# Attention's shift as a 33rd row of the score products, in a one-core four-layer hybrid kernel

## The chip, the cores and the metric

The kernel runs on one core of a Trainium2 chip. The core's engines each execute their own list of instructions in order: TensorE (PE, with its weight loads shown as PEld), VectorE (DVE), ScalarE (ACT), GpSimd (POOL) and SyncE (SP), which here only issues DMAs. They meet at semaphores. The metric is the device time of one execution in microseconds; less is better. The kernel before takes 6303.35 us, the median of three runs (6299.39, 6303.35 and 6311.23). A single-core kernel has no other cores to wait for.

## What is computed

An image batch (4, 32, 32, 256) passes through four layers; each batch element is a sequence of 1024 tokens of 256 channels.

- Layer 0: layer norm, projection to 512 channels, 3x3 depthwise convolution, a selective scan with 64 states per channel, projection back, plus the residual.
- Layer 1: a bottleneck block: 1x1, grouped 3x3 and 1x1 convolution.
- Layer 2: attention over a graph (8 heads of 32 channels, 1024 queries, 1024 keys, a mask made of the edges), then a mixture of 8 experts.
- Layer 3: a selective scan with 16 states per channel, then a second mixture of experts.

What matters here is the attention's core. For every head, query n and key k:

```
s[n, k] = q[n] . k[k] / sqrt(32)          # 32 channels
p[n, k] = exp(s[n, k] + mask[n, k] - m[n])   # m: a shift per query and head
out[n]  = sum_k p[n, k] v[k] / sum_k p[n, k]
```

The result doesn't depend on m. It only has to keep the exponential in range. The kernel bounds all scores by the norms of q and k; when the bound is under 40 it leaves m at zero, and only otherwise enters a branch that takes the true row maxima. With the inputs of this case no row maxima (`ps_sn` products) appear in the trace: the branch is skipped.

## The kernel before

**The scans.** The backbone is `scans` (line 384): 8 scans (4 batch elements in layer 0 and 4 in layer 3) in the order of `SCANS` (line 32), in all 1280 *units* of 128 rows by 1024 steps. A unit is: SP loads `dA` (512 KB, line 497), ACT takes its exponential, PE spreads the input over the states (`ps_rep`, 2 products), DVE multiplies by B and scans (`h`), POOL multiplies by C, and PE sums over the states (`ps_y`, 8 records for every 2 units). There are 5 `dA` buffers, so that SP issues the load of unit k+4 when the scan of unit k-1 has ended; `ps_rep` has 2 PSUM buffers.

**The side stages.** Everything else is a list of stages (`STAGES`, line 34): four `front`, four `middle` (end of layer 0, layer 1, attention, first experts, start of layer 3) and four `last` (end of layer 3 and second experts). Each is a Python generator that yields after a small piece of work. `run` (line 620) writes the program: between the halves of every unit it advances the current stage by pieces; `advance` (line 598) takes one stage at a time, and a stage starts when the one before it has been written out and the scan that it needs is done. What a stage hasn't finished when a scan needs its results is written out with no scan beside it (`need`, line 583, which sets `self.alone`).

**The pacing.** How many pieces go into a unit is decided by a clock per engine, `Metered` (line 99), which adds an estimate for every instruction as it is written. Pieces are added while no engine's clock is ahead of VectorE's:

```
if max(clock.values()) > clock["vector"] + LEAD or self.advance() is None:
    break
```

The estimate of a product is `matmul_us` (line 78): 0.46 ns per column, four times that for float32, a quarter for outputs of at most 32 rows, and half where the contraction has at most 32 rows:

```
if out.shape[0] <= 32:
    return us / 4
return us / 2 if lhsT.shape[0] <= 32 else us
```

**Attention's core.** `attention` (line 1264) normalizes and turns the tokens, projects them to `qT` and `kT` (channels on the 128 partitions, two chunks of 4 heads), bounds the scores (`large_scores`), loads the mask, makes `v`, and enters `shift`, the skipped branch. `mT` is the negated shift, zeros here: in bfloat16, where rows 0 to 2 of each head's 32 hold three parts of the float32 number. `all_heads` (line 1328) then walks 64 *steps* per batch element: 2 halves of the queries, 4 pairs of heads, 8 blocks of 128 keys. `scores` of step n is written after `values` of step n-2. A step's `scores` makes, for the two heads of the pair, one float32 product of 32 rows each (`ps_sc<-qT,kT`), adds the shift with one bfloat16 product of 32 rows each (`ps_sc<-mT,onesb`: ones times `mT`), adds the mask with one bfloat16 product of 128 rows each, and ACT exponentiates. `values` makes 4 float32 products with 32 output rows. A float32 product is two records in the trace. The two heads of a pair lie on neighbouring 32-row strips of the array. Where attention runs with no scan beside it, scores go to the scans' PSUM tile and are named `ps_sx`.

The order on each engine is the order in which the program was written; all SP transfers of scans and stages share one list.

Of the kernel before, what the change touches and what calls it, by code (L numbers as in the profile page):

```python
# [8 lines left out]
F32 = mybir.dt.float32  # L9
BF16 = mybir.dt.bfloat16  # L10
I32 = mybir.dt.int32
AF = mybir.ActivationFunctionType
ALU = mybir.AluOpType
# [4 lines left out]
P = 128  # L18
NB = 4
L = 1024  # L20
TB = L // P
C = 256
DI = 512
DC = DI // P
HEADS, HD = 8, 32
# [52 lines left out]
def matmul_us(out, lhsT=None, rhs=None, **_):  # L78
    if lhsT is None:
        lhsT = out  # L80
    us = 0.46e-3 * columns(out)
    if lhsT.dtype != BF16:
        us = max(4 * us, 0.3)
    if out.shape[0] <= 32:
        return us / 4
    return us / 2 if lhsT.shape[0] <= 32 else us


def by_columns(per, fixed, of=0):
# [53 lines left out]
class Hybrid:  # L143
# [1092 lines left out]
    def prepare2(self, st):  # L1236

        nc, vec = self.nc, self.vec
        self.gamma, self.beta, self.bo = (self.rows("L2_attn_" + n) for n in ("gamma", "beta", "bo"))
        wo = self.weight(st, "L2_attn_Wo", 2)  # L1240
        yield
        ps = self.ps("ps_bo", (P, C))
        for k in range(2):
            nc.tensor.matmul(
                ps, lhsT=vec["L2_attn_bv"][:, k : k + 1].to_broadcast([P, P]), rhs=wo[:, k, :],
                start=(k == 0), stop=(k == 1),
            )
        nc.vector.tensor_tensor(self.bo, self.bo, ps, ALU.add)
        self.isq = 1.0 / float(HD) ** 0.5
        self.bq = self.const.tile([P, 2], F32, name="bq_")  # L1250
        nc.vector.tensor_scalar(self.bq, vec["L2_attn_bq"], self.isq, None, ALU.mult)

        byhead = st.tile([P, 4], F32, name="byhead4")
        nc.vector.tensor_reduce(
            byhead, self.ident.rearrange("p (h d) -> p h d", d=HD), AX.X, ALU.add
        )
        self.byhead = self.const.tile([P, 4, 8], F32, name="byhead")
        nc.vector.tensor_copy(self.byhead, byhead.unsqueeze(2).to_broadcast([P, 4, 8]))
        self.onesb = self.const.tile([P, P], BF16, name="onesb")
        nc.vector.memset(self.onesb, 1.0)  # L1260
        self.ones = self.const.tile([P, 32], F32, name="ones32")
        nc.vector.memset(self.ones, 1.0)

    def attention(self, b, tb):
        nc, tc, vec = self.nc, self.tc, self.vec
        with tc.tile_pool(name=f"at{b}", bufs=1, side="right") as op:
            xa = op.tile([P, TB, C], F32, name="xa")
            qT = op.tile([P, 2, L], F32, name="qT")
            kT = op.tile([P, 2, L], F32, name="kT")
            v = op.tile([P, TB, C], F32, name="v")  # L1270
            mT = op.tile([P, 2, L], BF16, name="mT")
            maskT = op.tile([P, TB, L], BF16, name="maskT")
            wo = self.weight(op, "L2_attn_Wo", 2)
            large = op.tile([1, 1], I32, name="large")
            nc.vector.memset(mT, 0.0)
            with tc.tile_pool(name=f"aa{b}", bufs=1, side="right") as fp:
                wq, wk, wv = (self.weight(fp, "L2_attn_" + n, 2) for n in ("Wq", "Wk", "Wv"))
                xT = fp.tile([P, 2, L], F32, name="xTa")
                yield from self.norm(fp, tb, TB, xa, "lnt")
                yield from self.turned(xa, TB, xT)  # L1280

                def project(item):
                    w, dst, bias, sc, c, g = item
                    ps = self.ps("ps_qk")
                    cols = slice(g * 512, (g + 1) * 512)
                    self.mm(ps, lambda k: w[:, k, c * P : (c + 1) * P], xT, 2, cols)
                    nc.scalar.activation(
                        dst[:, c, cols], ps, AF.Identity, bias=bias[:, c : c + 1], scale=sc
                    )

                yield from self.pipe(
                    [
                        (w, dst, bias, sc, c, g)
                        for w, dst, bias, sc in (
                            (wq, qT, self.bq, self.isq), (wk, kT, vec["L2_attn_bk"], 1.0)
                        )
                        for c in range(2) for g in range(2)
                    ],
                    project, cost=1.7,
                )  # L1300

                yield from self.large_scores(fp, qT, kT, large)
                for _ in self.mask_work:
                    pass
                nc.sync.dma_start(maskT, self.mem[("maskT",)].rearrange("j p f -> p j f"))

                def values(j):
                    ps = self.ps("ps_v", (P, 2, C))
                    for i in range(2):
                        m = 2 * j + i  # L1310
                        for k in range(2):
                            nc.tensor.matmul(
                                ps[:, i, :], lhsT=xT[:, k, m * P : (m + 1) * P], rhs=wv[:, k, :],
                                start=(k == 0), stop=(k == 1),
                            )
                    nc.scalar.copy(v[:, 2 * j : 2 * j + 2, :], ps)

                yield from self.pipe(range(TB // 2), values, cost=1.7)
            go = nc.values_load(large, engines=self.sides, min_val=0, max_val=1)
            tc.mark_branch_hint_location(f"large{b}", go, engines=self.sides)  # L1320
            yield from self.add_rows(xa, self.bo, TB)
            yield from self.add_rows(tb, self.beta, TB)
            with tc.tile_pool(name=f"ab{b}", bufs=1, side="right") as fp:
                yield from self.shift(fp, qT, kT, mT, maskT, go, f"large{b}")
            with tc.tile_pool(name=f"ac{b}", bufs=1, side="right") as fp:
                yield from self.all_heads(b, fp, tb, qT, kT, v, maskT, mT, xa, wo)

    def all_heads(self, b, fp, tb, qT, kT, v, maskT, mT, xa, wo):
        nc = self.nc

        def divided(raw, sums, c):
# [8 lines left out]
        halves = [  # L1340
            [fp.tile([P, 2, 512], F32, tag=t, name=t, bufs=2) for t in ("raw", "sums")]
            for _ in range(2)
        ]
        scores, values = self.heads(fp, halves, qT, kT, v, maskT, mT)
        for n in range(len(steps) + 2):
            if n >= 2:
                values(steps[n - 2])
# [69 lines left out]
    def row_max(self, fp, qT, kT, mT, mask):  # L1417
# [1 line left out]

        nc = self.nc  # L1420

        m3 = fp.tile([P, TB, HEADS, 32], BF16, name="m3")
        nc.vector.memset(m3, 0.0)
        mx = fp.tile([P, TB, HEADS, 2], F32, name="mx")
        got = {}
        yield 1.0
# [29 lines left out]
        )  # L1456
        m = fp.tile([P, TB, HEADS], F32, name="mneg")
        nc.vector.tensor_reduce(m, mx, AX.X, ALU.max, negate=True)
        for s in range(3):
            nc.vector.tensor_copy(m3[:, :, :, s], m)  # L1460
            if s < 2:
                nc.vector.tensor_tensor(m, m, m3[:, :, :, s], ALU.subtract)
        yield 1.0

        def turn(item):
            c, g = item
            ps = self.ps("ps_m3", dtype=BF16)
            for k in range(4):
                nc.tensor.transpose(
                    ps[:, k * P : (k + 1) * P],  # L1470
                    m3[:, 4 * g + k, 4 * c : 4 * c + 4, :].rearrange("p h s -> p (h s)"),
                    self.identb,
                )
            nc.scalar.copy(mT[:, c, g * 512 : (g + 1) * 512], ps)

        yield from self.pipe([(c, g) for c in range(2) for g in range(2)], turn, cost=0.8)

    def heads(self, fp, halves, qT, kT, v, maskT, mT):

        nc = self.nc
        got, acc = {}, {}

        def scores(step):
            nh, hp, kb = step
            qs = slice(nh * 512, (nh + 1) * 512)
            c, at = hp // 2, 64 * (hp % 2)
            alone = self.alone  # L1490
            if alone:
                both = self.scan_psum.tile([P, 2, 512], F32, tag="x", name="ps_sx", bufs=2)
                two = [both[:, i, :] for i in range(2)]
            else:
                two = [self.psum.tile([P, 512], F32, tag="s", name="ps_sc", bufs=2) for _ in range(2)]
            rows = [slice(at + 32 * i, at + 32 * i + 32) for i in range(2)]
            for i in range(2):
                nc.tensor.matmul(
                    two[i], lhsT=kT[rows[i], c, kb * P : (kb + 1) * P], rhs=qT[rows[i], c, qs],
                    start=True, stop=False,  # L1500
                )
            for i in range(2):
                nc.tensor.matmul(
                    two[i], lhsT=self.onesb[rows[i], :], rhs=mT[rows[i], c, qs],
                    start=False, stop=False,
                )
            got[step] = p = fp.tile([P, 2, 512], F32, tag="p", name="p", bufs=3)
            for i in range(2):
# [659 lines left out]
```

## Time and profile before

| what | value |
|---|---|
| median of three runs | 6303.35 us |
| profiled execution | 6294.21 us, its span 6292.5 us |
| mean granted TensorE clock | 0.842 |
| PE busy | 5142.7 us, 82% |
| DVE busy | 5032.7 us, 80% |
| POOL, ACT busy | 3825.9 us (61%), 3410.6 us (54%) |
| attention steps of elements 0, 1, 2 | 1400 to 1645, 2462 to 2704, 3826 to 4072 us |
| attention steps of element 3 | 5192 to 5234 us beside the last units of scan (3, 2), 5234 to 5388 us alone |
| stage `last 0` ends, `middle 2` begins | 3617.25 us, 3622.86 us |
| stage `last 1` ends, `middle 3` begins | 4985.39 us, 4990.77 us |

All times inside the execution are counted from the start of the span. All instructions that the pacing meters are recorded at line 131 of the helper, so they are told apart by their tiles: "ps_sc<-qT,kT" is what writes `ps_sc` from `qT` and `kT`, "32*128 32x512 f32 x4" is 4 records with 32 rows of weights, 128 columns, and a moving operand of 32 by 512. A view of stretches lists the busy time of each engine and its record count in each, then the granted clock, the DMA share and GB/s.

### The profile page before, as it was taken

Reading aid. Unit: us, or ns where it says so; the run is one execution under the profiler, and the core shown is the slowest. Engines: PE = TensorE matmul, PEld = TensorE weight load, DVE = VectorE, ACT = ScalarE, POOL = GpSimd, SP = SyncE. Lnnn points to the kernel's source line nnn. Section 1 sums busy time; section 2 is a strip of 40 time slices with the busy share of each in tenths; the row PEclk is TensorE's granted clock in tenths of the full one; section 3 lists DMA queues with packets and bytes.
Section 4 is the critical chain, followed back from the end, with each engine's and each line's share of the span. In section 5 each row is a group of like instructions: output and inputs, shape, how many; then the busy total and the mean of one; then the engine's idle time right before and its main releaser. Section 6 shows DMA issues by size and latency. Waiting matters only on the chain. (4 is left out here: it accounts for less than half of the span.)

```text
span 6292.5 us, 59823 instructions
## 1 busy us (share of the span) xinstructions
PE 5142.7 (82%) x20249; PEld 2117.1 (34%) x20249; DVE 5032.7 (80%) x4016; ACT 3410.6 (54%) x4299; POOL 3825.9 (61%) x1948
## 2 busy tenths in 40 slices
PE   5676785579798568979869969989689779997999
PEld 2122120132253122234225522244145332543566
DVE  5888898988898998889889988899889982317811
ACT  3565655345496435558638735567547544336621
POOL 2787768665586766568767756577867752006600
PEclk7687785589798668979969979979779889999989
DMA  3555555544355656445455576345545761027611
GB/s 109 160 158 167 165 175 185 159 150 136 113 173 177 194 165 170 132 128 191 159 178 174 182 179 165 119 150 195 174 156 179 208 161 48 19 73 184 166 34 34
DMA packets 347915, 934.97 MB, mean 149 GB/s; under 512 B 37748, under 2 KB 120256, under 8 KB 345984
## 3 DMA queue, kind: packets, MB, share of 16 engines
q1 hardware_dynamic: 344880, 928.38, 48.7%
q0 software_dynamic: 2128, 2.13, 0.2%
q8 instruction: 165, 2.70, 0.2%
q14 instruction: 166, 1.36, 0.1%
q10 hardware_dynamic: 576, 0.39, 0.0%
HBM read 841.02 MB, written 92.37 MB: 148 GB/s over the span
## 5 line engine op out<-in xcount | busy, mean ns | idle before, releaser
L131 POOL TENSOR_TENSOR h<-h,rows 128x1024 f32<-128x1024 f32 x1280 | 3024.2, 2366 | 1740.4 <-DVE h L131 1529.3
L131 DVE TENSOR_TENSOR_SCAN h<-dA,ps_rep 128x1024 f32<-128x1024 f32 x1280 | 2924.3, 2285 | 182.2 <-ACT dA L131 53.6
L131 DVE TENSOR_TENSOR ps_rep<-ps_rep,rows 128x1024 f32<-128x1024 f32 x1280 | 1549.4, 1210 | 142.6 <-PE ps_rep L131 141.7
L131 PE MATMUL ps_rep<-S,spread_L_conv_A_log 96*128 96x512 bf16 x2048 | 752.8, 456 | 770.3 <-DVE h L131 722.4
L131 ACT ACTIVATE dA<-dA,A_L_conv_A_log 128x1024 f32<-128x1024 f32 x1024 | 1125.4, 1142 | 440.0 <-DMA dA<-dt 405.7
L131 PE MATMUL ps_y<-h,collect_L_conv_A_log 128*32 128x512 f32 x4096 | 704.4, 741 | 15.3 <-POOL h L131 15.3
L131 PE MATMUL ps_e<-we,h_m 128*128 128x256 f32 x3072 | 709.4, 383 | 8.3 <-ACT h_m L131 8.3
L131 PEld LDWEIGHTS <-spread_L_conv_A_log 96*128 96x128 bf16 x2048 | 159.7, 102 | 1558.0 <-DVE h L131 1246.4
L131 PEld LDWEIGHTS ps_e<-we,h_m 128*128 128x128 f32 x3072 | 583.3, 191 | 159.2 <-ACT h_m L131 31.0
L131 PE MATMUL ps_h<-xTm,we 128*128 128x512 f32 x1280 | 603.3, 607 | 4.6 <-DMA we<-in_L_ffn_W_dram 4.5
L131 ACT ACT_TABLE_LOAD x402 | 515.8, 1283 | 37.0 <-PE ps_h L131 15.5
L131 ACT ACTIVATE h_m<-ps_h,cols 128x512 f32<-128x512 f32 x384 | 257.5, 686 | 423.0 <-PE ps_h L131 421.0
L131 ACT ACTIVATE p<-ps_sc 128x512 f32<-128x512 f32 x404 | 219.3, 594 | 316.7 <-PE ps_sc L131 306.1
L131 ACT ACTIVATE dA<-dA,A_L_attn_A_log 128x1024 f32<-128x1024 f32 x256 | 282.8, 1143 | 141.4 <-DMA dA<-dt 122.8
L131 PEld LDWEIGHTS ps_h<-xTm,we 128*128 128x128 f32 x1280 | 242.2, 193 | 281.0 <-issue 211.5
L131 PE MATMUL ps_rep<-S,spread_L_attn_A_log 96*128 96x512 bf16 x512 | 176.8, 433 | 160.2 <-DVE h L131 138.6
L131 PE MATMUL ps_at<-p,v 128*32 128x512 f32 x1024 | 270.7, 608 | 0.2 <-ACT p L131 0.2
L131 PE MATMUL ps_at<-p,ones 128*32 128x512 f32 x1024 | 270.7, 608 | 0.0
L131 DVE SCALAR_TENSOR_TENSOR tb_rows<-ps_e,cw,tb_rows 128x256 f32<-128x256 f32 x128 | 55.7, 477 | 242.8 <-PE ps_e L131 242.7
L131 PE MATMUL ps_sc<-qT,kT 32*128 32x512 f32 x808 | 244.0, 654 | 4.6 <-ACT p L131 2.0
L131 PE MATMUL ps_cv<-pad,diag 128*128 128x512 f32 x504 | 230.5, 597 | 0.0
L131 PEld LDWEIGHTS ps_y<-h,collect_L_conv_A_log 128*32 128x32 f32 x4096 | 93.2, 118 | 339.7 <-issue 216.6
(347 smaller groups left out, 5475.6 us busy)
## 6 DMA issues: line engine op xcount, KB each, us to landing
dA<-dt SPq DMA_DIRECT2D x1280, 512.0 KB
we<-in_L_ffn_W_dram SPq DMA_DIRECT2D x64, 512.0 KB
parts<-parts SPq DMA_DIRECT2D x60, 384.0 KB
S<-parts SPq DMA_DIRECT2D x90, 256.0 KB
dt<-sp_r SPq DMA_DIRECT2D x64, 256.0 KB
y<-yo SPq DMA_DIRECT2D x128, 128.0 KB
y_back<-y SPq DMA_DIRECT2D x64, 256.0 KB
we<-in_L_ffn_w_dram SPq DMA_DIRECT2D x64, 256.0 KB
```

The source lines that it names most:

```text
L131: return got(*args, **kw)
```

## The change

1. The shift becomes a 33rd row of the score product: k gets a row of ones, q a row that holds the negated shift in float32. The ones product, `onesb` and the three-part bfloat16 `mT` go. A step's `scores` is then two float32 products of 33 rows and the two mask products.
2. The heads' rows are laid out in DRAM: `k_rows` and `q_rows`, 33 rows of 1024 per head and batch element. In `prepare2` four transfers write the row of ones. In `attention` sixteen transfers of 32 rows by 1024 (128 KB) store q and k after the projections and before `large_scores`; one of 8 rows (32 KB) stores `mT` after the branch.
3. `heads` loads them back two heads at a time: `load` issues four transfers (two of 132 KB for k, two of 66 KB for q) into tiles where one head lies on partitions 0 to 32 and the other on 64 to 96, with two buffers. The first pair and the second are loaded in front of step 0, each later one a pair ahead.
4. `qT`, `kT` and `mT` live in an inner pool that is released before `all_heads`; the skipped branch makes 8-row transposes.
5. `matmul_us` halves the estimate for contractions of up to 64 rows, which the 33-row products alone meet besides those that had the half before.

```diff
-    return us / 2 if lhsT.shape[0] <= 32 else us
+    return us / 2 if lhsT.shape[0] <= 64 else us
...
-        self.onesb = self.const.tile([P, P], BF16, name="onesb")
-        nc.vector.memset(self.onesb, 1.0)
+        one = st.tile([HEADS, L], F32, name="one_row")
+        nc.vector.memset(one, 1.0)
+        self.k_rows = [self.keep(("k", b), [HEADS, HD + 1, L]) for b in range(NB)]
+        for to in self.k_rows:
+            nc.sync.dma_start(to[:, HD, :], one)
...
+                    for x, to in ((qT, self.q_rows(b)), (kT, self.k_rows[b])):
+                        for h in range(HEADS):
+                            at = HD * (h % 4)
+                            nc.sync.dma_start(to[h, :HD, :], x[at : at + HD, h // 4, :])
+                    yield from self.large_scores(fp, qT, kT, large)
...
                 with tc.tile_pool(name=f"ab{b}", bufs=1, side="right") as fp:
                     yield from self.shift(fp, qT, kT, mT, maskT, go, f"large{b}")
+                nc.sync.dma_start(self.q_rows(b)[:, HD, :], mT)
             with tc.tile_pool(name=f"ac{b}", bufs=1, side="right") as fp:
-                yield from self.all_heads(b, fp, tb, qT, kT, v, maskT, mT, xa, wo)
+                yield from self.all_heads(b, fp, tb, v, maskT, xa, wo)
...
+        def load(nh, hp):
+            k = fp.tile([P, L], F32, tag="k_rows", name="k_rows", bufs=2)
+            q = fp.tile([P, 512], F32, tag="q_rows", name="q_rows", bufs=2)
+            for i in range(2):
+                at = slice(64 * i, 64 * i + HD + 1)
+                nc.sync.dma_start(k[at, :], self.k_rows[b][2 * hp + i])
+                nc.sync.dma_start(q[at, :], self.q_rows(b)[2 * hp + i, :, nh * 512 : (nh + 1) * 512])
+            rows[nh, hp] = k, q
...
-            rows = [slice(at + 32 * i, at + 32 * i + 32) for i in range(2)]
+            if kb == 0:
+                at = 4 * nh + hp
+                for g in range(0 if at == 0 else at + 1, min(at + 2, 8)):
+                    load(g // 4, g % 4)
+            k, q = rows[nh, hp]
             for i in range(2):
+                of = slice(64 * i, 64 * i + HD + 1)
                 nc.tensor.matmul(
-                    two[i], lhsT=kT[rows[i], c, kb * P : (kb + 1) * P], rhs=qT[rows[i], c, qs],
-                    start=True, stop=False,
-                )
-            for i in range(2):
-                nc.tensor.matmul(
-                    two[i], lhsT=self.onesb[rows[i], :], rhs=mT[rows[i], c, qs],
-                    start=False, stop=False,
+                    two[i], lhsT=k[of, kb * P : (kb + 1) * P], rhs=q[of, :], start=True, stop=False
                 )
```

## The prediction

> **What bounds the kernel now.** I first read the page's slices.
>
> ```profile
> PE   5676785579798568979869969989689779997999
> ...
> DVE  5888898988898998889889988899889982317811
> ```
>
> VectorE is at 8 or 9 tenths, so the scans set the pace, except in the 34th to 36th slice and the last two: there it falls to 3 and less while PE stays at 9. The first of these gaps is the end of `middle 3`, which scan (3, 3) waits for; the second is the last experts. What shortens PE's work in the first is gained whole. Next the stretches (busy time of PE, PEld, DVE, ACT, POOL; then the clock, DMA share and GB/s).
>
> ```profile
> 1100.00:1220.00 120.00, 66.79 (x204) 7.79 (x204) 115.50 (x68) 39.31 (x35) 80.00 (x34) 0.50 0.53 166
> 1400.00:1645.00 245.00, 241.32 (x1376) 64.85 (x1380) 215.39 (x137) 140.04 (x207) 149.87 (x68) 0.99 0.41 130
> ...
> 5192.00:5234.00 42.00, 41.44 (x205) 10.96 (x204) 26.78 (x16) 17.96 (x29) 23.33 (x12) 0.81 0.24 58
> 5234.00:5388.00 154.00, 154.00 (x879) 38.90 (x871) 14.43 (x19) 64.92 (x73) 22.30 (x18) 1.00 0.14 33
> ```
>
> With no stage beside it a unit takes 120/34 = 3.53 us (34 scans lie in the first stretch), nearly all DVE. In attention PE is busy 241 of 245 us and DVE only 215: **in all four attentions PE is the bound**, beside the scans (second and third row) and alone (last). VectorE's groups in the second stretch give the pace:
>
> ```profile
> L131 DVE TENSOR_TENSOR_SCAN h<-dA,ps_rep 128x1024 f32<-128x1024 f32 x59 | 134.9, 2286 | 11.2 <-ACT dA L131 5.5 <-DVEq L1411 0.2
> ```
>
> 64 steps over 59 units: 1.085 steps a unit, 4.14 us a unit. Then PE in order of time, one step with no scan beside it:
>
> ```profile
> 5301.87 1.13 PE L131 MATMUL ps_sx<-qT,kT 32*128 32x512 f32 x4
> 5302.84 0.38 PE L131 MATMUL ps_sx<-mT,onesb 32*128 32x512 bf16 x2
> 5303.15 0.60 PE L131 MATMUL ps_sx<-maskT,identb 128*128 128x512 bf16 x2
> 5303.69 0.62 PE L131 MATMUL ps_at<-p,v 128*32 128x512 f32 x2
> ...
> 5304.68 0.70 PE L131 MATMUL ps_sx<-qT,kT 32*128 32x512 f32 x2
> ```
>
> From start to start: score pair 0.97 us, ones pair **0.31**, mask 0.54, values 0.99; a step is 2.81. And a unit's own share, beside a step:
>
> ```profile
> 1481.24 0.60 PE L131 MATMUL ps_rep<-S,spread_L_conv_A_log 96*128 96x512 bf16 x2
> 1481.77 1.13 PE L131 MATMUL ps_sc<-qT,kT 32*128 32x512 f32 x4
> ...
> 1483.58 1.06 PE L131 MATMUL ps_y<-h,collect_L_conv_A_log 128*32 128x512 f32 x8
> 1484.47 0.60 PE L131 MATMUL ps_at<-p,v 128*32 128x512 f32 x2
> ```
>
> 0.53 for `ps_rep` and 0.89 every second unit for `ps_y`: 0.97 a unit. Check: 64 x 2.81 + 59 x 0.97 = 237.0; the steps last 244.3 us (1400.6 to 1644.9), and the other 7.3 are the output projection and the cold start.
>
> **The ones product goes.** 0.31 us a step, 256 steps, all on PE where PE is the bound: 79 us at most.
>
> **The score pair gets 33 rows.** The trace has no product of 33 to 64 rows beside another. Its bounds: the 32-row pair, 0.97, where both heads run at once; and one after the other, 2 x 0.86 (a full float32 product: `ps_h` in the chain, 16 records in 6.87 us) + 0.12 = 1.84. No reading of the trace makes it cheaper than 0.97. The Trainium skill, TensorEngine Tiling (Array Packing), section Overview, gives contractions of up to 64 rows a factor of up to two, and its Tiling Modes list two tiles of 64 rows. Partitions 0 to 32 and 64 to 96 fall into different ones. By that rule the step becomes 2.50 us; without it 3.37. I take 0.97, the nearest row: it too has two heads on separate strips.
>
> **The pacing.** Its estimates by step were 0.94 (scores) + 0.24 (ones) + 0.47 (mask) + 0.94 (values) = 2.59; they become 2.35. With the new 64-row limit the pair keeps its half. So 1.085 x 2.59/2.35 = 1.19 steps go into a unit, and 64 steps take 54 units, five fewer. A unit's PE work is 0.97 + 1.19 x 2.50 = 3.95, still over 3.53: PE remains the bound.
>
> **What five units are worth.** After `middle 0` the stages end long before the next scan, so five units at 3.53 return. From `middle 1` on they follow each other without a gap: `last 1` ends at 4985.39, `middle 3` begins at 4990.77, 48 us and 14 units after scan (0, 3) has ended (counting scans, unit 1152, the first of scan (3, 2), starts at 4942). So attentions 1 and 2 hand five units each to `middle 3`; its steps begin ten units earlier, with 17 instead of 7 units of scan (3, 2) left. Some 22 steps instead of 10 lie beside scans, and 42 instead of 54 alone.
>
> **The new transfers.** Sixteen stores of q and k before `large_scores`, SP's 0.55 us each, are 8.8 us on SP, and `maskT` and the `dA` loads queue behind them. SP waits there anyway, from 1363.85 to 1370.40 for a scan and to 1379.82 for `y`, and a `dA` load has two units (7 us) until ACT takes its exponential. I cost them at 1 us in all; without that cover 5 us an attention, because scores' exponentials queue behind `dA` on ACT and PE waits for those. The loads of later pairs (four, 2.2 us of SP in 8 steps, after a wait for PE's last product of the buffer's old pair) cost nothing while `dA` has its 3 us to spare; if that is gone, 2 us for some 24 pairs. The four transfers of ones and the larger memset: 1 us. All new bytes, 21 MB, are 2% of what is moved.
>
> **The first pair is the new wait.** SP stores `mT`, waits for that store, because the q loads read its row, and only then issues what step 0 waits for. SP issues four loads, then the second pair's; every `dA` load after them waits, and on PE `ps_rep` of the next units waits behind step 0. Today SP leaves the branch at 1399.99 and step 0 starts at 1400.66, so nothing covers the chain. Two rows for a transfer, a 512 KB load on SP's queue, with ACT's wait that it ends, and a tiny scatter (last column, issue to landing):
>
> ```profile
> 1392.27 0.51 SPq L497 DMA_DIRECT2D dA<-dt  x1
> ```
>
> ```profile
> 1396.17 1.15 ACT L131 ACTIVATE dA<-dA,A_L_conv_A_log 128x1024 f32<-128x1024 f32 x1 [2.35 <-DMA dA<-dt]
> ```
>
> ```profile
> mask_dram<-zero,where POOLq DMA_INDIRECT x64, 2.2
> ```
>
> 3.9 and 2.2 us. Store from 1400.3; the fourth load starts 1.7 after the store has landed, and lands: delay 5.8 us by the small row, 9.2 by the large. The skill speaks against such chains: DMA: Bandwidth & Descriptors, Rules for kernel authors, calls transfers below 64 KB mostly overhead, and its Anatomy of one DMA fits 2.0 us + bytes/436e3 for GpSimd's transfers, so an estimate of 2.1 to 2.3 here: 5.7 us. I take **7** for each of four starts, nearer the small row, as 32 to 132 KB are. Below nothing it can't be.
>
> **Doubled steps.** Where two steps fall into a unit, the second pair waits for exponentials (1.1 us against 0.99 of values between): I put 2 us on each attention, between 0 and 4.
>
> **The sum**, against the span of 6292.5:
> - Attention beside scans, new: 64 x 2.50 + 54 x 0.97 + 7.3 + 7 + 2 = 228.7, against 244.3.
> - Element 0: 228.7 + 5 x 3.53 = 246.4: +2.1. Elements 1 and 2: -15.6 each.
> - Element 3 beside scans: 22 x 2.50 + 17 x 0.97 + 7 + 1 and the 7 us that today's 42 have beyond 10 x 2.81 + 7 x 0.97: 86.5, +44.5. Alone: 42 x 2.50 = 105 against 54 x 2.81 = 151.7: -46.7.
> - Stores and setup +2.
>
> 2.1 - 31.2 + 44.5 - 46.7 + 2 = **-29 us**: span 6263, 0.46% less. The profiled execution is 9 us under the median of the runs; the same share of 6303.35 gives 6274.
>
> **Rivals.**
> - *The five units aren't handed on* (the program's order leaves 59 units, or `middle 3` begins where it did). For: the pacing's other clocks may hold. Against: 1.085 is what PE's clock alone gives. Then elements 0 to 2 cost +2.1 each, element 3 +4 beside scans and -16.7 alone; with +2: -4 us, 6299.
> - *The start is longer*: each us counts four times. With 14 us instead of 7, -1 us: 6302; with 18, 6318. For: `dA` loads share the queue. Against: both rows above.
> - *Slower: the 33-row pair doesn't share the array.* Place: every `scores`; price 0.87 us. Elements 0 to 2: 2.1 + 55.7, then twice -15.6 + 55.7; element 3: 44.5 + 19.1 and 141.5 - 151.7; with +2 the sum is +193 us: 6497. It decides from 29/256 = 0.11 us: a pair over 1.08 us makes the kernel slower. For: no such product in the trace. Against: the 32-row pair shares.
>
> **The numbers.** Forecast 0.54, units not handed on 0.13, longer start 0.13, no sharing 0.14, others (a shifted order that collides elsewhere) 0.06. About 0.2% (12.6 us) is what a measurement of this kernel can tell from no change. Faster: 0.54, 0.03 of the second, 0.02 of others: 0.59. Slower: 0.14, 0.05 of the long start, 0.03: 0.22. Same: 0.19. The forecast's own range is 6250 (start 5.7, no doubled-step loss, four more units handed on) to 6289. The range given, 6235 to 6320, takes in the next two cases and leaves no sharing out.
>
> **What would show it.** Right: a score pair near 0.97 and a step of 2.50 us in the alone stretch; about 54 scans in each of the first three attentions; `middle 3` some 35 us earlier; about 42 `ps_sx` exponentials instead of 54; PE idle some 7 us ahead of the first step. Wrong: a pair near 1.8; ACT's waits for `dA` growing inside attention; DVE's waits for `ps_rep` growing by more than the start.

## The result, and the profile after

The changed kernel takes 6355.03 us (median of four runs, 6344.78 to 6358.41), the kernel before 6301.64 in runs on the same chip (6299.39 to 6311.23): a ratio of **1.0074** (95% interval 1.0061 to 1.0087), so 53 us slower where I had forecast 29 us faster, and outside the range of 6235 to 6320. The profiled execution has a span of 6355.1 us, 62.6 more than the one before. One execution of a kernel can differ from the next by some 10 us, so below a place is read from the traces and a total from the medians, against the kernel before in runs on the same chip.

The lines that answer those of before: slices of the page; then the stretches (busy time of PE, PEld, DVE, ACT, POOL; then clock, DMA share, GB/s), which are the steps of element 0, the steps of element 3 beside scans, and alone.

```profile
PE   6676785579798567979869968979679779897999
...
DVE  5888898988898997889889987889889985217811
```

```profile
1413.00:1650.00 237.00, 228.28 (x1212) 58.75 (x1234) 193.46 (x124) 134.27 (x202) 133.18 (x61) 0.96 0.41 135
5251.00:5346.00 95.00, 90.98 (x460) 22.73 (x470) 65.58 (x37) 49.07 (x75) 47.74 (x22) 0.90 0.42 108
5346.00:5451.00 105.00, 103.23 (x560) 25.22 (x566) 11.07 (x18) 48.55 (x56) 20.60 (x17) 1.00 0.22 60
```

VectorE's first gap (34th to 36th slice) begins part of a slice later. The stretch alone is 105 us, where it was 154, as forecast (by luck, see below). But the steps of element 0 still last 236 us for only 52 units, PE's busy time is 228 instead of 241, and its granted clock is 0.96 where it was 0.99. VectorE's groups of that stretch, the second of them as it was before, and PE in order of time alone:

```profile
L131 DVE TENSOR_TENSOR_SCAN h<-dA,ps_rep 128x1024 f32<-128x1024 f32 x53 | 121.1, 2284 | 9.0 <-ACT dA L131 3.8
L131 DVE TENSOR_TENSOR ps_rep<-ps_rep,rows 128x1024 f32<-128x1024 f32 x52 | 63.4, 1220 | 28.8 <-PE ps_rep L131 28.6
```

```profile
L131 DVE TENSOR_TENSOR ps_rep<-ps_rep,rows 128x1024 f32<-128x1024 f32 x59 | 71.6, 1214 | 11.2 <-PE ps_rep L131 11.2
```

```profile
5400.95 1.13 PE L131 MATMUL ps_sx<-q_rows,k_rows 33*128 33x512 f32 x4
5402.01 0.60 PE L131 MATMUL ps_sx<-maskT,identb 128*128 128x512 bf16 x2
...
5403.55 1.13 PE L131 MATMUL ps_sx<-q_rows,k_rows 33*128 33x512 f32 x4
```

52 scans instead of 59 lie beside the steps, and VectorE waits 28.6 us for PE where it waited 11.2. The 33-row pair shares the array: it takes 1.06 us, not the estimated 1.84. A step alone is 2.60 here (median over the stretch 2.593, before 2.807).

The time between fixed scans shows where the loss is (scans counted from 0; each stretch begins a dozen units ahead of an attention and ends behind it, the last with the first scan of (3, 3), which waits for the end of `middle 3`):

| stretch | before | after | |
|---|---|---|---|
| scan 280 to 400 (element 0) | 510.7 | 535.5 | +24.8 |
| 536 to 656 (element 1) | 507.9 | 538.5 | +30.6 |
| 856 to 976 (element 2) | 521.0 | 541.6 | +20.6 |
| 1136 to 1216 (element 3) | 794.7 | 765.8 | -28.9 |
| all the rest | 3958.2 | 3973.7 | +15.5 |

Of the rest, 6.0 us arise at one place in the setup (scans 20 to 22), and 7.3 between scans 656 and 856, where `middle 2` now begins six units earlier. Element 0 splits like this: the first step comes 12.8 us later, two scans further on (5.9 of it since scan 280); the steps take 9.3 us less, with seven scans fewer; and the 50 scans behind them take 28.1 us more than the 45 did, where five units more are worth 17.7. So 10.4 us are lost **behind** the steps, at a place that the prediction didn't look at.

### The profile page after: what moved, and what is told of

Same layout as the page of the kernel before. It is cut to its first block, busy times and chain, and to the rows that moved or that the text cites. A ratio compares the mean times of both kernels' runs of the same rounds, so it can differ in the third digit from the quotient of the medians.

```text
span 6355.1 us, 59095 instructions
## 1 busy us (share of the span) xinstructions
PE 5102.3 (80%) x19653; PEld 2094.3 (33%) x19737; DVE 5041.6 (79%) x4016; ACT 3405.8 (54%) x4314; POOL 3827.4 (60%) x1948
## 5 line engine op out<-in xcount | busy, mean ns | idle before, releaser
L131 ACT ACTIVATE p<-ps_sc 128x512 f32<-128x512 f32 x434 | 235.4, 595 | 355.3 <-PE ps_sc L131 262.7
L131 PE MATMUL ps_sc<-q_rows,k_rows 33*128 33x512 f32 x868 | 274.3, 667 | 37.1 <-DMA k_rows<-k 21.9
```

The source lines that it names most:

```text
L131: return got(*args, **kw)
```

## The experiments

**Pacing alone.** In the kernel before:

```diff
-    return us / 2 if lhsT.shape[0] <= 32 else us
+    if lhsT.shape[0] <= 32:
+        return 0.0 if lhsT.dtype == BF16 else us / 2
+    return us
```

> The kernel before, scores and ones product as they were, with the ones product's estimate set to nothing. That gives exactly the program order of the changed kernel: steps over the same units (52 in the first three attentions, scores from the 298th, 554th, 876th and 1198th scan on), the same order of the norm behind them. Theory 'pacing' (what was lost comes from the order that the estimates write: fewer scans beside attention, two steps in one unit, and the attention's end falling so that VectorE's norm statistics wait for POOL): each of the first three elements +25 to +30 us, of it 10.4 behind the steps (one unit of 11.4 us where it was 4.4), in all 6362 us (6345 to 6380). Rival 'rows' (what was lost comes from the transfers, the start of the first pair and the new products): only the prediction's own accounting is left, 52 units instead of 59 and 25 steps beside the last scans: +15 us, 6318.

Measured: 6330.15 against 6305.0, ratio 1.0041 (1.0026 to 1.0055): +25 us, nearly half of the loss, with no row and no transfer. The first three stretches of the table cost +21.1, +17.3 and +10.2. My 6362 was too much and the rival's 6318 too little. The unit behind the steps that takes 11.4 us in the changed kernel takes 4.9 here, **with the same order of instructions**: so the order alone doesn't make that wait.

**The rows at the old pacing.** In the changed kernel:

```diff
-    return us / 2 if lhsT.shape[0] <= 64 else us
+    if 32 < lhsT.shape[0] <= 64:
+        return 0.628 * us
+    return us / 2 if lhsT.shape[0] <= 32 else us
```

> The changed kernel with the estimate of a product of 33 to 64 rows raised from 0.5 to 0.628 of the full one, so that a step costs the planner 2.59 us again as before: 58 units an attention, scores from the 298th, 554th, 882nd and 1210th scan on. The rows, their transfers and the 33-row pair stay. Theory 'pacing': steps 64 x 0.22 us shorter, the start 8 us later, setup +6; the norm behind the attention comes in a third order. 6291 if that costs nothing, up to 6320 if it costs what the changed kernel's order does. Rival 'rows': the loss stays, 6340 or more.

6330.62 against 6305.0, ratio 1.0046 (1.0026 to 1.0065): +26. So each half of the change costs by itself about what the other does. The long unit behind the steps is here too (9.7 us), and in the next kernel.

**The place of the norm.**

```diff
+        for _ in range(1):
+            yield 0.0
         yield from self.finished(b, fp, tb, 1, halves[1][0], xa, wo)
```

> The changed kernel with one empty turn of the planner put between the last step of an attention and its output projection. Steps stay in the units where they were in the first two attentions; the norm's statistics come behind the next unit's multiplication again, as in the kernel before; the third and fourth attention begin 2 and 4 units later. If the order of the norm costs 10.4 us an element: -31 and +10 for four fewer scans beside the last attention: 6334 us, and the unit of 11.4 us is gone. If that unit is only where a delay from elsewhere shows: 6355 to 6365, the 11.4 us turning up in a unit beside it.

6342.98, +38. The order of the norm is that of the kernel before, and still the unit takes 9.8 us. The expectation fell: what these kernels share, and the pacing alone doesn't have, is the rows' layout of SBUF. q, k and the shift (by their shapes 20480 bytes of each partition) moved into a pool that is closed ahead of the steps, so that the pool of the steps shifts into that space. If it now reaches into the space that the next layer's pool takes over, the first tile there has to wait for the last readers of the old pool, POOL's sums among them. The next run tests this.

**A gap of 7936 bytes.** An unused tile pushes the pool of the steps away from that space again, though not all the way back to where it lay before:

```diff
+            with tc.tile_pool(name=f"gap{b}", bufs=1, side="right") as gp:
+                gp.tile([P, 1984], F32, name="gap")
-            with tc.tile_pool(name=f"ac{b}", bufs=1, side="right") as fp:
-                yield from self.all_heads(b, fp, tb, v, maskT, xa, wo)
+                with tc.tile_pool(name=f"ac{b}", bufs=1, side="right") as fp:
+                    yield from self.all_heads(b, fp, tb, v, maskT, xa, wo)
```

> The changed kernel with an unused tile of 7936 bytes a partition above the pool of the steps, so that this pool lies where it lay in the kernel before, clear of the next layer's first tiles. No instruction is added. If VectorE's 6.3 us wait for POOL at the end of each of the first three attentions comes from the next norm's tiles taking over space of the pool that POOL still reads: that unit falls from 11.4 to 4.9 us (as in the run of the pacing alone), 3 x 6.4 = -19 us, 6336. If it comes from the order of the norm's instructions: no change, 6355.

6321.95 against 6302.17, ratio 1.0025 (1.0015 to 1.0036): 33 us less than the changed kernel. POOL and VectorE in order of time in the changed kernel, then VectorE in this one:

```profile
1682.17 1.26 POOL L131 TENSOR_TENSOR tb<-tb,y_at 128x512 f32<-128x512 f32 x1
1683.46 0.43 DVE L131 BATCH_NORM_STATS2 lnm_st<-tb 128x6 f32<-128x256 f32 x1 [6.33 <-POOL tb L131]
```

```profile
1664.64 2.29 DVE L131 TENSOR_TENSOR_SCAN h<-dA,ps_rep 128x1024 f32<-128x1024 f32 x1
1666.84 0.40 DVE L131 BATCH_NORM_STATS2 lnm_st<-tb 128x6 f32<-128x256 f32 x1
```

The statistics start right behind the scan, the unit takes 4.93 us, and the scans behind the steps take 6.7, 6.4 and 6.7 us less in the first three elements: 20 us are traced to the gap. The other 13 I can't place; in its profiled execution 7 us lie ahead of the first attention's steps, where the instructions are the same, so they may be chance.

**A smaller tile of ones.**

```diff
-        one = st.tile([HEADS, L], F32, name="one_row")
+        one = st.tile([64, P], F32, name="one_row")
...
-            nc.sync.dma_start(to[:, HD, :], one)
+            nc.sync.dma_start(to[:, HD, :].rearrange("h (a x) -> h a x", x=P), one)
```

> The changed kernel with the row of ones as a tile of 64 x 128 (512 bytes a partition) in place of 8 x 1024 (4 KB), written to the same rows of k. If the 5.4 us that SP waits at 216 us for a store of the parts come from where the tile of 4 KB pushes the next weights in SBUF: SP issues these weights at once again, the 21st scan is at most 1.5 us later than in the kernel before (now 5), total 6350. If the memset and the four transfers cost it: the 21st scan stays 4 to 5 us late, 6355.

SP in order of time, changed kernel, then this one:

```profile
215.50 0.55 SPq L709 DMA_DIRECT2D parts<-parts  x1
221.59 0.38 SPq L251 DMA_DIRECT2D w_L_conv_w_out<-in_L_conv_w_out_dram  x1
```

```profile
213.65 0.55 SPq L709 DMA_DIRECT2D parts<-parts  x1
214.29 0.44 SPq L251 DMA_DIRECT2D w_L_conv_w_out<-in_L_conv_w_out_dram  x1
```

This fits the same mechanism: the 4 KB of ones moved the weights onto a buffer that a transfer of `parts` was still using, for which SP waits in the changed kernel. With 512 bytes the wait of 5.4 us is gone, and scan 23 is where it was before (0.08 us earlier; 5.5 later in the changed kernel). The total, 6354.58, doesn't show it: in the profiled execution this kernel is still 8.4 us ahead of the changed one at scan 400, and the lead is gone by scan 1216; what took it back was not traced. A cause of 4 to 5 us can be seen in the trace and not in these totals.

**The start.**

```diff
+                    nc.sync.dma_start(self.q_rows(b)[:, HD, :], mT)
                     for x, to in ((qT, self.q_rows(b)), (kT, self.k_rows[b])):
...
-                nc.sync.dma_start(self.q_rows(b)[:, HD, :], mT)
...
             for _ in self.row_max(fp, qT, kT, mT, maskT):
                 pass
+            nc.sync.dma_start(to[:, HD, :], mT)
```

> The changed kernel with the shift's row written to q's rows before q and k are stored, and once more inside the branch only (where the branch isn't taken the row is zero as before). Pacing and program order of the steps stay. If the store of the row and the wait for it set the start: the first exponential of an attention comes 2.5 to 3.5 us sooner behind the branch (now 10.5 us behind it in the first element, 2.6 in the kernel before), four times: -10 to -14 us, 6343. If the eight loads themselves set it: less than 1 us each, 6355.

6341.02 against 6302.17, ratio 1.0055: -14 against the changed kernel. From VectorE's first scan behind the branch to the first exponential it is 1.9, 1.8, 3.4 and 3.2 us before, 9.8, 10.3, 11.3 and 10.7 after, and 7.2, 8.4, 9.3 and 8.4 here. The wait for the small store is worth 2.2 us a start, a bit less than expected, so 9 of the 14 us; the larger part of the start is left with the eight loads. SP and PE in the changed kernel:

```profile
1407.46 0.33 SPq L1333 DMA_DIRECT2D q<-mT  x1
1410.43 0.29 SPq L1495 DMA_DIRECT2D k_rows<-k  x1
...
1413.10 0.35 SPq L1496 DMA_DIRECT2D q_rows<-q  x1
1413.42 3.34 PE L131 MATMUL ps_sc<-q_rows,k_rows 33*128 33x512 f32 x4 [6.50 <-DMA k_rows<-k]
```

The store lets go after 2.97 us (the prediction's estimates had 2.1 and 2.2, its large row 3.9), the loads are issued at one per 0.39 us, and the first pair itself lasts 3.3 us. The second pair, at the same half clock, lasts 2.6; that the rest is the second head's rows landing later is likely and not shown.

**The pair, with 32 rows.**

```diff
-                of = slice(64 * i, 64 * i + HD + 1)
+                of = slice(64 * i, 64 * i + HD)
```

> The changed kernel with the score products contracting only the 32 rows of q and k, on the same two strips (partitions 0 to 31 and 64 to 95): the shift's row is left out. Everything else stays, the loads of 33 rows too. Alone a step is 2.59 us in the changed kernel, where the prediction had 2.50. If the 33rd row costs the difference: pair 0.97, step 2.50, some -15 to -23 us in all, 6335. If the two strips lying 64 apart, or the mask's product right behind the pair, cost it: the step stays at 2.59 and the time at 6355.

6356.91; the step alone has a median of 2.591 us. The 33rd row costs nothing.

**No ones product, no rows.** In the kernel before, the two products of the ones taken out, and the estimate of the pair raised:

```diff
-            for i in range(2):
-                nc.tensor.matmul(
-                    two[i], lhsT=self.onesb[rows[i], :], rhs=mT[rows[i], c, qs],
-                    start=False, stop=False,
-                )
...
-    return us / 2 if lhsT.shape[0] <= 32 else us
+    return us * 0.628 if lhsT.shape[0] <= 32 else us
```

> The kernel before without the ones product (the shift is left out), q and k in the old layout, the score pair's estimate raised to 0.628 so that a step costs the planner the same 2.59 as before: 58 units an attention. No new transfer, no row. It is the most that taking the ones product away can bring at this pacing. The prediction's step: 2.50 alone (2.81 - 0.31). If the pair on neighbouring strips takes 0.97 and only the distance of 64 costs the 0.09: step 2.50 alone. If the 0.09 belongs to the change from the pair to the mask's full product, whatever stands in front of it: step 2.59 alone. Beside scans by the prediction 64 x 0.31 = 20 us an element, -79 in all: 6225. If VectorE sets the pace of the 16 steps beside the first half's division and norm, and a step saves 0.22 elsewhere at most: 8 to 11 us in elements 0 to 2, 12 in the last, and 3.5 back for one unit fewer: 6260 to 6275.

6283.09 against 6300.77, ratio 0.9976 (0.9966 to 0.9985): -18 us, and no more. PE alone:

```profile
5301.34 1.13 PE L131 MATMUL ps_sx<-qT,kT 32*128 32x512 f32 x4
5302.40 0.61 PE L131 MATMUL ps_sx<-maskT,identb 128*128 128x512 bf16 x2
```

The pair ahead of the mask takes 1.06 here too, on the old strips: distance and rows are out of it, and the 0.09 goes with whatever stands in front of the mask's full product. So the ones product was worth 0.22 us, not 0.31. And beside scans even that does not come through: the first three stretches of the table are 510.2, 513.0 and 522.0 us (-0.5, +5.1, +1.0), the last is 775.2 (-19.5). **Taken out alone, the ones product gains nothing beside the scans.** In groups of eight steps, element 0 goes from 119.4 to 114.2 us in the first four groups and from 56.4 to 55.4 in the last two; in the fifth and sixth, which lie beside the first half's division and norm, from 67.9 to 71.5, with one scan more (3.5). So some of it is gained in the first half and given back in the sixth group, where PE now runs dry for 2.3 us and then at half its clock (last section): of PE's work the lower clock takes 5.1, 4.7 and 4.6 us there in elements 0 to 2, and nothing in the kernel before. (What the lower clock takes, here and below, is PE's busy time times what the granted clock lacks to 1.00.)

**Element 0 stretched.** If each scan beside the steps costs 0.97, stretching them over more scans where nothing is handed on must gain. In the kernel before, in `scores`:

```diff
+            if b == 0:
+                self.clock["tensor"] += 0.45
```

> The kernel before with 0.45 us added to TensorE's planned time for each step of element 0 only: its steps go over 68 scans instead of 57, one step a unit; elements 1 to 3 keep their order. After element 0 the stages wait for the next scan anyway, so nothing is handed on and each unit beside the steps costs about 0.97 instead of 3.54. If the count of units beside the steps is what pacing costs: 11 x 2.57 = -28 less 4 for VectorE, which then sets the pace: 6278. If two steps in a unit or the norm's place are the cost: 6303, as before.

6302.29, ratio 1.0003 (0.9991 to 1.0015). The steps take 287.7 us over 69 scans: ten scans more cost 42 us, 4.2 each, not 0.97. So the linear sum of PE's work doesn't hold in that direction. Of the 32 us too much, 19 are the lower clock (it takes 22.3 us in these steps, 3.3 before) and some 12 are PE's idle time (14.6 us, 3.0 before): with less to do in each unit PE runs dry more often, and it works more of the time at half clock. The same on the repaired rows (gap, start, ones, and 0.7 us for element 0):

> The changed kernel with the gap, the early row of the shift, the small tile of ones, its own pacing, and 0.7 us added to the planned time of each step of element 0 only (69 scans instead of 52). Against the changed kernel: -33 (gap), -14 (start), and 15 to 17 units x 2.57 = -35 to -40 less what VectorE takes: 6355 - 80 = 6275, faster than the kernel before. If the rows lose more beside scans than these parts: 6300.

6300.71, ratio 1.0002: level with the kernel before, not 25 us under it, and 14 us under the same kernel without the stretch (the next run), for 17 scans more. Its steps of element 0 take 283.0 us over 69 scans.

**The repairs together**, first at the change's pacing, then at the old one:

> The changed kernel with the gap, the early row of the shift and the small tile of ones, pacing untouched. If these parts add up: 6355 - 33 - 14 = 6308, and 20 to 25 us under the kernel before at the same pacing (6330), which is what the rows are then worth. If they overlap: 6320.

6315.07 against 6300.77, ratio 1.0022 (1.0009 to 1.0035): 40 us under the changed kernel, and against the kernel before +14 where pacing alone costs +25.

> The rows at the old pacing (estimate 0.628), the gap, the small tile of ones and the early row of the shift together. Against the run of the rows at the old pacing (span 6341): -5 for the setup, -19 for the norm's wait, -12 for the start: span 6305, about the kernel before. If the loss of the rows at the old pacing lies elsewhere (the loads of the later pairs, VectorE's own work): 6325 or more.

6301.19 against 6302.17, ratio 0.9994 (0.9987 to 1.0002): no difference.

**VectorE's stand.** In the sixth group VectorE waits 5.2 to 7 us for ScalarE's inverse root, which queues behind exponentials. Two empty turns of the planner let scans in between:

```diff
         nc.scalar.activation(r, r, AF.Exp, scale=-0.5)
+        for _ in range(2 if tag == "lny" else 0):
+            yield 0.0
         w = pool.tile([P, n], F32, tag=tag + "_w", name=tag + "_w")
...
-        r = self.rstd(pool, mv[:, :, 1], 1e-5, n, tag)
+        r = yield from self.rstd(pool, mv[:, :, 1], 1e-5, n, tag)
```

> The kernel before with two empty turns of the planner between ScalarE's two activations of an attention norm (the inverse root) and VectorE's correction of them, so that one or two scans stand between them on VectorE instead of a wait of 7 us. If VectorE sets the pace there: 5 to 7 us less in each of the first three attentions, 6301 - 18 = 6283. If TensorE does: less than 2 us each, 6300.

> The kernel before without the ones product (the shift is left out, estimate 0.628) and with the same two turns. If the stand of VectorE is what took the saving: the groups of 16 steps shorten by 5 to 7 us an element, 6283 - 18 = 6265. If TensorE's own clock and order took it: 6280.

> The repaired rows at the old pacing with the same two turns. If VectorE sets the pace of those 16 steps: 6301 - 18 = 6283, faster than both kernels. If TensorE does: 6300.

The kernel before becomes slower: 6321.11 against 6302.79, ratio 1.0027 (1.0016 to 1.0038). Without the ones product it gains: 6261.70, 0.9937 (0.9920 to 0.9954), 21 us under the same kernel without the turns. The repaired rows gain too: **6287.76, ratio 0.9976 (0.9966 to 0.9987)**, faster than both kernels, with the shift in place (its branch isn't entered with these inputs). VectorE's waits over the whole run (in all, times, longest), kernel before, then with the turns; then the kernel without the ones product, with the turns:

```profile
DVE ps_rep L131 <- PE ps_rep L131: 141.7, 104, 7.7
...
DVE lny_w L131 <- ACT lny_r L131: 39.6, 8, 16.7
```

```profile
DVE ps_rep L131 <- PE ps_rep L131: 164.2, 110, 9.5
...
DVE lny_w L131 <- ACT lny_r L131: 17.2, 2, 16.7
```

```profile
DVE ps_rep L131 <- PE ps_rep L131: 137.4, 84, 7.6
...
DVE lny_w L131 <- ACT lny_r L131: 15.9, 2, 15.4
```

In the kernel before, 22.4 us of one wait become 22.5 us of the other: PE was the next limit. Without the ones product 17.8 of 33.7 us go, the waits for PE don't grow (142.0 before the turns), and the sixth group of element 0 falls from 34.7 us with seven scans to 27.4 with six. About 5 of the 7 us are the clock: with the turns PE doesn't run dry there, and the lower clock takes nothing in this group, where it took about 5 us. In the kernel before it took nothing there anyway. Only both changes together are worth more than the parts.

Not all of this is cleared up. By the traces the turns take 5.0, 5.2 and 6.5 us from the first three stretches of the kernel without the product. Another 10 us less between scans 656 and 856, and 21 us more in the last stretch, go with elements 2 and 3 starting two and four units later; in all these two executions differ by 7 us, where the medians differ by 21. That the turns make the kernel before slower by 18 us stays open too. In the profiled execution 10.1 us lie in element 1, and there the lower clock takes 8.8 us of PE's work in the steps, against nothing before: they begin at half clock, with PE idle for only 0.5 us directly ahead of them. Whether that is so in the other executions is not on record.

| kernel | us, against before on the same chip |
|---|---|
| the change | +53 |
| pacing alone | +25 |
| rows at the old pacing | +26 |
| the change with the gap | +20 |
| the change without the start's store | +39 |
| the change, all three repairs | +14 |
| repairs, old pacing | -1 |
| no ones product, no rows | -18 |
| repairs, old pacing, the two turns | -15 |
| before, the two turns | +18 |
| no ones product, no rows, the two turns | -41 |

The repaired rows at the old pacing lie 17 us behind the kernel without the product, and 26 with the turns. The part of the start that no repair removed is of that size (33.3 us in four starts with the early store, 10.3 in the kernel before), but no run takes it away.

## Why the prediction was wrong

Three terms of the sum failed. The 79 us of the ones product were 18 when it was taken out alone. The new pacing, whose units the forecast's own rates put at +15, measured +25. And the new places of the tiles in SBUF, which cost 20 us in three places and 6 in the setup by the traces, had no term at all. By the medians, and in this order, the 53 us are: +25 for the pacing; -11 for the rows at that pacing once they are repaired (+14 instead of +25); and +39 for what the repairs took away (+53 to +14). At the old pacing the same repairs take away 27 us, all that the rows cost there. By the steps of the prediction:

- **"0.31 us a step, all on PE where PE is the bound"** failed twice. The size is 0.22 (2.807 to 2.593 alone; 2.59 in three layouts): the 0.09 was not the ones product's. And PE was not the only bound beside scans: the kernel without the product gains nothing there, and its 18 us lie in element 3. The sum took PE's work at full clock and back to back. With less work PE runs dry in the sixth group of steps, where VectorE waits for ScalarE, and then works at half clock; with the turns, which end that wait, the same kernel gains 41 us.
- **The 33-row pair** shares the array, as forecast: 1.06 us for both heads, against an estimate of 1.84 one after the other. The rule of the Trainium skill (TensorEngine Tiling (Array Packing), Overview: up to a factor of two for contractions of up to 64 rows) held, with 1.7 against that estimate. The rival without sharing is out.
- **The pacing**: 52 units, not 54, and `middle 3` 12 units earlier in the order, not ten. But with every unit of the attentions longer, it starts 48 us later in time, where the forecast had it 35 us earlier. The forecast's worth of units (3.53 where they return, 0.97 beside the steps) gave +15 us for this pacing alone; it measured +25. Some 4 us of the difference in element 0 lie behind the steps, where the order of the norm is new (21.9 us for five scans more, instead of 17.7).
- **The start**: 7 us were put in; 7.9 measured to the first exponential. The cold start inside its 7.3 us was left as it was; in the steps of the first three elements the lower clock took 3.3, 0.0 and 4.6 us before and 9.5, 9.5 and 7.8 after. That the new idle time causes this is not shown (last section).
- **"Stores and setup +2"**: the sixteen stores are hidden, as forecast (scans 280 to 297 take as long as before, scans 528 to 552 grow by 2.4 us). The setup costs 6.0, for a reason that isn't in the list of instructions: where the tile of ones lies.
- **What no step had**: the pools moved. 6.4 to 6.7 us in each of three places are shown by the gap, and stood in none of the rivals. The prediction cost every instruction and every transfer, and no address.
- **Element 3 alone** came out at the forecast 105 us by luck: 39 steps of 2.69 instead of 42 of 2.50, two misses that cancel.
- **Doubled steps** (2 us) were not measured by themselves.

## What to carry to other kernels

A busy share of 98% says that an engine is a bound, not that it is the only one: before a saving is counted whole, take the work out of the old kernel and see what that alone gives, and compare the granted clock before and after: an engine with less work can run slower. When a change moves or adds tiles, ask which pool's space the next stage's first tile takes over, and who still reads there; the wait appears in a line that the change doesn't touch. And in a planned kernel, an estimate that is made smaller is a change of its own; run it alone.

## What the runs showed of the hardware

**At the start of the steps.** PE's clock, changed kernel at the start of element 1 (columns as above), then the kernel before at the same place:

```profile
2490.00:2496.00 6.00, 3.94 (x12) 0.47 (x12) 5.79 (x4) 3.04 (x3) 6.00 (x4) 0.50 0.92 215
2496.00:2502.00 6.00, 0.00 (x0) 0.00 (x0) 5.70 (x3) 0.41 (x1) 4.92 (x3) 0.50 0.52 150
2508.00:2514.00 6.00, 6.00 (x18) 1.06 (x17) 0.50 (x1) 1.09 (x2) 0.00 (x0) 0.50 0.00 0
2514.00:2520.00 6.00, 6.00 (x26) 1.03 (x22) 3.02 (x2) 1.65 (x3) 2.36 (x1) 0.62 0.00 0
```

```profile
2462.00:2468.00 6.00, 5.53 (x26) 1.72 (x26) 5.70 (x3) 2.17 (x4) 6.00 (x5) 1.00 0.60 173
```

While the rows load PE has nothing to do for 6 us, and then works at half its clock until about 2518.5: 16 us from the first product, of which the last ten are without any gap. Before, the steps of this element began at full clock. The Trainium skill, TensorE: Matmul & The Clock Gate, Part 1, puts the way back to full clock at about 3.4 us of sustained work; here it took 10 us, and the measurement decides. Some 8 us are lost so (15.6 us of work at half the clock).

The 6 us of idle time are not shown to be the cause. The clock had been at half since 2481, ahead of them (first row). In the kernel before, the steps of elements 2 and 3 begin at half clock too, with PE idle for only 0.3 us directly ahead of them, and reach full clock 9.5 and 15.5 us after the first product. In the traces of the eleven kernels with rows all 44 starts are at half clock, in those of the six without rows 17 of 24.

**Inside the steps.** The kernel without the ones product behind VectorE's wait in element 1, then the kernel before at the same place:

```profile
2636.00:2640.00 4.00, 1.68 (x8) 0.24 (x4) 3.52 (x6) 3.42 (x6) 0.52 (x1) 0.82 0.00 0
2640.00:2644.00 4.00, 4.00 (x13) 0.71 (x12) 4.00 (x4) 0.05 (x1) 1.83 (x1) 0.50 0.41 131
```

```profile
2636.00:2640.00 4.00, 1.99 (x17) 0.42 (x8) 3.90 (x4) 2.04 (x2) 0.98 (x1) 1.00 0.01 4
2640.00:2644.00 4.00, 3.83 (x22) 0.88 (x20) 3.76 (x4) 2.83 (x6) 2.76 (x2) 1.00 0.44 141
```

PE is idle for 2.3 us in the first kernel and for 2.0 us in the second. In the first its clock falls to half before the idle stretch ends and stays there for 10.2 us, though PE works without a gap from 2639.4 us on; in the second it doesn't fall. It is the same in elements 0 and 2 of both.
